# Attention energies as full-array float32r matmuls: keys and queries in two halves, keys read back from DRAM for every unit

## The chip, the core and the metric

The kernel runs on one core of a Trainium2 chip. The metric is device time in microseconds (us), from the first to the last instruction of the core. A core has TensorE (PE in the profile; PEld is its weight load), VectorE (DVE), ScalarE (ACT), GpSimd (POOL) and SyncE (SP, which here only issues transfers), and 16 DMA engines that all queues share.

## The reference: what is computed

Two layers on a tensor x of 4 images, 64 x 64 pixels, 256 channels, all in float32. The first is self-attention over the 4096 pixels of each image, with keys and queries of only 32 channels. The second is a DCNv3 block (layer norm, depthwise convolution, deformable sampling in 16 groups with 9 points each, projection) and an MLP with 1024 hidden channels. The change lies in the first layer:

```python
q = x @ wq + bq            # (4, 4096, 32)
k = x @ wk + bk            # (4, 4096, 32)
v = x @ wv + bv            # (4, 4096, 256)
energy = jnp.einsum('bnd,bmd->bnm', q, k)
attention = jax.nn.softmax(energy, axis=-1)
x_out = jnp.einsum('bnm,bmc->bnc', attention, v)
return gamma * x_out + inputs
```

## The kernel before, in words

**Tiling.** The work is cut into 64 *units* of 256 query pixels, 16 for each of the 4 images. For a unit, the energies of its 256 queries with all 4096 keys are made in 4 groups (`energies(g)`, line 743) of 8 matmuls, each for 128 keys x 256 queries with a contraction of 32 channels. A group fills four PSUM tiles `e0` to `e3` of 128 x 512. ScalarE turns them into exponentials (`exponentials`, line 756, four activations a group), without the row maximum. `weighted` (line 768) then multiplies the exponentials with the values V of the 4096 keys and accumulates the 256 x 256 result in PSUM; a column of ones in V gives the sum that the softmax divides by (`front`, lines 791 to 797).

**Keys and queries.** `project(b, u)` makes keys, queries and values of the 256 pixels of unit u of image b. `wkq` holds the weights of keys and queries side by side, in two orders, one for even and one for odd u, so that one pair of matmuls (`pkq`, line 651) gives keys and queries on the partitions where they are wanted. `key_bias` adds the bias on ScalarE: two activations of 32 x 128 put the keys into one of the four 32-partition strips of `kTs` (line 659), and one of 32 x 256 makes the queries (line 665), which SP writes to DRAM (`qd`, line 666). `kTs` has two sets of tiles in SBUF: while the units of one image are worked on, the other set receives the keys of the next image. `Attention.load` reads a unit's queries back four times, once for each strip (line 707). So four energies at a time run in four strips of 32 rows of the array.

**Other stages.** Around the attention, each unit passes `front` (residual, layer norm, input projection `pp`, line 825, written to DRAM as `xp`), `plan` (convolution, offsets and masks: the matmuls `po` at line 909, VectorE's `om` at line 918), `sample` (5 rows `win` of `xp` from DRAM, line 1068, weighted on VectorE, line 1088) and `back` (output projection `pout`, line 1169, then the MLP: `ph`, line 1194, and `pmlp`, line 1211). Several units are under way at once.

**Order.** The order of the work on TensorE, VectorE, ScalarE and GpSimd is written out by hand: every step has a due time in the table `WHEN` (a unit's period is T = 60 there), with other times for the last units in `LATE`. `whole` sorts all steps by due time and emits them; within an engine they run in that order. SP's transfers are not under that order; the framework places them. For the first image all 16 projections run ahead of the first unit; the projections for image b + 1 run during image b, one per unit.

A second version of the main loop (`general=True`, with `largest`) subtracts the row maximum and is only run when a check at the end finds values out of range. It was not run here.

Of the kernel before, what the change touches and what calls it, by code (L numbers as in the profile page):

```python
# [7 lines left out]

F32 = mybir.dt.float32
I32 = mybir.dt.int32  # L10
AF = mybir.ActivationFunctionType
ALU = mybir.AluOpType
AX = mybir.AxisListType
# [3 lines left out]
def tile_attention_dcnv3_block(  # L17
# [23 lines left out]
    nc = tc.nc  # L41
    B, H, W, C = x.shape
    N = H * W
    P = 128
# [88 lines left out]
    raw = p1.tile([P, C // P, 2, CQ], F32, tag="cv", name="raw_qk")  # L133
    for i, w in enumerate((wk, wq)):
        nc.sync.dma_start(raw[:, :, i, :], w.rearrange("(k p) m -> p k m", p=P))
    wkq, bkq = [], []
    for odd in range(2):
        t = const.tile([P, C // P, 4, CQ], F32, name=f"wkq{odd}")
        v = const.tile([P, 1], F32, name=f"bkq{odd}")
        for r in range(4):  # L140
            i = (r // 2 + odd) % 2
            nc.vector.tensor_copy(t[:, :, r, :], raw[:, :, i, :])
            nc.scalar.dma_start(v[r * CQ : (r + 1) * CQ, :], (bk, bq)[i].rearrange("(p o) -> p o", o=1))
        wkq.append(t.rearrange("p k r m -> p k (r m)"))
        bkq.append(v)
    wv_s = weight(wv, "wv_s", True)
    bv_s = bcast(bv, C, "bv_s", True)
    gamma_s = bcast(gamma, 1, "gamma_s")
# [174 lines left out]
    def rows4(r):  # L323
        return slice(r * CQ, (r + 1) * CQ)
# [293 lines left out]
    def project(b, u):  # L618


        n = f"{b}_{u}"
        first = b == 0
        odd = u % 2
        st = {}

        def load():
            if first:
                xs = p8.tile([P, 2, C], F32, tag="ex", name=f"xs_{n}")
            else:
                xs = p1.tile([P, C // P, 256], F32, tag="xs", name=f"xs_{n}")  # L630
            st["xs"] = xs
            if first:
                nc.sync.dma_start(xs, xt_[b, u])
            else:
                in_blocks(xs, xs_, b * N + 256 * u, 2)

        def turn():
            st["pt"] = transposed(st["xs"], f"x_{n}", 2, *((ps_e, f"e{odd}") if first else ()))

        def copy():  # L640
            st["xT"] = p3.tile([P, C // P, 256], F32, tag="cT", name=f"xT_{n}")
            if first:
                nc.scalar.copy(st["xT"], st["pt"])
            else:
                nc.vector.transpose(st["xT"].rearrange("p k t -> p (k t)"), st["xs"].rearrange("p k t -> p (k t)"))

        def keys():
            pool, tag = (ps_e, f"e{2 + odd}") if first else (ps, "m")
            st["pkq"] = pkq = pool.tile([P, 256], F32, tag=tag, name=f"pkq_{n}")
            for k in range(C // P):  # L650
                nc.tensor.matmul(  # L651
                    pkq, lhsT=wkq[odd][:, k, :], rhs=st["xT"][:, k, :], start=(k == 0), stop=(k == 1)
                )
# [36 lines left out]
        if not first:  # L690
            del d["turn"]
        return d
# [5 lines left out]
    class Attention:  # L698
        def __init__(self, b, u, general):
            self.b, self.u, self.general, self.n = b, u, general, f"{b}_{u}"  # L700
            self.ex = {}
            self.kT = kTs[b % 2]

        def load(self):
            self.qs = p2.tile([P, 256], F32, tag="qs", name=f"qs_{self.n}")
            for r in range(4):
                nc.sync.dma_start(self.qs[rows4(r), :], qd[self.b * NU + self.u])
            self.x = p2.tile([P, 2, C], F32, tag="x1", name=f"x1_{self.n}")
            nc.sync.dma_start(self.x, xt_[self.b, self.u])

        def e_tile(self, r, name):
            return ps_e.tile([P, 2, 256], F32, tag=f"e{r}", name=f"{name}_{self.n}")

        def largest(self):

            n, qs = self.n, self.qs
            self.nm = p2.tile([P, 256], F32, tag="qT", name=f"nm_{n}")
            for i in range(2):
                mxs = sm.tile([P, NT], F32, tag="mxs", name=f"mxs_{n}_{i}")
                for t in range(NT):  # L720
                    e = self.e_tile(t % 4, f"em_{i}_{t}")[:, 0, :P]
                    nc.tensor.matmul(
                        e, lhsT=qs[rows4(t % 4), i * P : (i + 1) * P], rhs=self.kT[t // 4][rows4(t % 4), :],
                        start=True, stop=True,
                    )
# [3 lines left out]
                nc.vector.tensor_scalar(  # L729
                    spread.rearrange("p (r c) -> p r c", c=CQ)[:, :, 0],  # L730
                    mx.to_broadcast([P, 4]), -1.0, None, ALU.mult,
                )
                pm = ps.tile([P, P], F32, tag="m", name=f"pm_{n}_{i}")
                nc.tensor.matmul(pm, lhsT=spread, rhs=ident, start=True, stop=True)
                nc.vector.tensor_copy(self.nm[:, i * P : (i + 1) * P], pm)

        def energies(self, g):
            if g == 0 and self.general:
                self.largest()
            self.es = es = [self.e_tile(r, f"e_{g}_{r}") for r in range(4)]  # L740
            for jj in range(2):
                for r in range(4):
                    nc.tensor.matmul(  # L743
                        es[r][:, jj, :], lhsT=self.kT[2 * g + jj][rows4(r), :], rhs=self.qs[rows4(r), :],
                        start=True, stop=not self.general,
                    )
                    if self.general:
                        nc.tensor.matmul(
                            es[r][:, jj, :], lhsT=every[rows4(r), :], rhs=self.nm[rows4(r), :],
                            start=False, stop=True,  # L750
                        )

        def exponentials(self, g):
            for r in range(4):
# [641 lines left out]
    def whole(general):  # L1396
        shifted.clear()
        wns, sps = {}, {}
        steps = []

        def put(slot, stage, some, later=0.0):
            late = LATE.get(stage, {}).get(slot, {})
# [4 lines left out]
        for b in range(B):  # L1407
            for u in range(NU):
# [11 lines left out]
                if general and u == 0:  # L1420
                    put(s, "general", {"e0": some.pop("e0"), "x0": some.pop("x0")})
                put(s, "attention", some)
                put(s, "tables", {k: lambda f=f: ready(f) for k, f in TABLES.items()})
# [96 lines left out]
```

## Time and profile before

| | |
|---|---|
| three runs, us | 3818.03, 3818.6, 3821.02 (median 3818.6) |
| profiled execution: span, us | 3820.9 (the page gives no other time of it) |
| energies (line 743), TensorE busy, us | 296.3 in 4096 records |
| weighted values (line 768), TensorE busy, us | 1902.2 in 8192 records |
| granted TensorE clock, mean over the span | 0.996 |
| DMA | 378.04 MB, 99 GB/s on average |
| spacing of units: images 1 to 3 / last image, us | 57.77 / 55.19 |

The page describes one profiled execution. Busy times are per engine; a record is one instruction. A float32 matmul shows as two records on PE and two on PEld. Matmuls are pipelined, so a record's duration is longer than the distance to the next one, and costs on TensorE are read as distances between starts. In a timeline line stand: start in us, duration in us, engine, line, operation, output <- inputs, shapes, number of records merged, and in brackets the idle time before it and what ended it.

### The profile page before, as it was taken

What the parts mean: (1) busy time and instruction counts of PE and PEld (TensorE: products, weight loads), DVE (VectorE), ACT (ScalarE), POOL (GpSimd) and SP (SyncE); (2) the same over time, 40 slices, a digit from 0 to 9 for tenths busy, and PEclk for the clock granted to TensorE, in tenths of its full rate; (3) what the DMA queues carried; (4) which work ended last, traced back from release to release, by engine and by line L of the source; (5) the groups of instructions that cost most, each with busy time, mean ns of one, the idle gap of its engine ahead of it and who ended that gap; (6) DMA issues with size and microseconds to landing.
All of it is one profiled execution on the core that took longest, in us unless ns stands there. A gap on an engine that the chain in (4) does not pass through costs nothing.

```text
span 3820.9 us, 56101 instructions
## 1 busy us (share of the span) xinstructions
PE 3773.3 (99%) x20274; PEld 3124.5 (82%) x20274; DVE 3422.7 (90%) x6247; ACT 2175.1 (57%) x4213; POOL 313.1 (8%) x444
## 2 busy tenths in 40 slices
PE   8999999999999999999999999999999999999988
PEld 7788888888888888888888888888888888888867
DVE  2599999999999999999999999999999999999995
ACT  4455555565565565565565565565565665555443
POOL 1000000000000000000000000000000000000021
PEclk9999999999999999999999999999999999999999
DMA  5333333334343333433534333333344333333331
GB/s 151 91 92 95 101 89 96 101 90 140 99 115 89 105 92 91 107 92 91 150 90 114 102 90 97 99 92 98 101 125 108 95 83 94 91 86 82 93 89 51
DMA packets 320111, 378.04 MB, mean 99 GB/s; under 512 B 133488, under 2 KB 270256, under 8 KB 319824
## 3 DMA queue, kind: packets, MB, share of 16 engines
q1 hardware_dynamic: 309728, 367.47, 35.5%
q10 hardware_dynamic: 8512, 3.43, 0.4%
q8 instruction: 162, 2.65, 0.3%
q0 software_dynamic: 1584, 3.47, 0.3%
q14 instruction: 125, 1.02, 0.1%
HBM read 251.69 MB, written 122.56 MB: 98 GB/s over the span
## 4 chain that ended last, share of the span: by engine, by line
PE 96%; DVE 3%; DMA 0%; ACT 0%; issue 0%; SPq 0%; ACTq 0%; DVEq 0%
PE acc L768 46%; PE ph L1194 12%; PE pmlp L1211 11%; PE e L743 7%; PE po L909 5%; PE pout L1169 3%; PE pp L825 3%; PE pv L672 3%; PE pkq L651 1%; PE pt_s L331 1%; PE pt_p L331 1%; PE pc L885 1%; DVE pw L1088 1%; PE pt_f L331 1%; PE pt_b L331 1%; DVE cv L872 1%
## 5 line engine op out<-in xcount | busy, mean ns | idle before, releaser
L768 PE MATMUL acc<-V,ex 128*128 128x257 f32 x8192 | 1902.2, 382 | 0.2
L768 PEld LDWEIGHTS acc<-V,ex 128*128 128x128 f32 x8192 | 1536.8, 190 | 267.4 <-issue 64.8
L1088 DVE TENSOR_TENSOR pw<-win,wn 128x1280 f32<-128x1280 f32 x640 | 933.2, 1484 | 9.5 <-ACT wn L1032 1.9
L1096 DVE TENSOR_TENSOR pw<-pw,pw 128x1280 f32<-128x1280 f32 x492 | 730.6, 1485 | 0.1
L756 ACT ACTIVATE ex<-e 128x512 f32<-128x512 f32 x1024 | 529.2, 603 | 64.5 <-PE e L743 55.7
L1194 PE MATMUL ph<-hT_b,f1w 128*128 128x256 f32 (+1 forms) x2080 | 494.0, 380 | 5.2 <-ACT hT_b L311 2.3
L1211 PE MATMUL pmlp<-f2w,gT 128*128 128x256 f32 x2048 | 462.7, 379 | 1.3 <-DVE x1b L1176 1.1
L1194 PEld LDWEIGHTS ph<-hT_b,f1w 128*128 128x128 f32 x2080 | 382.3, 190 | 81.9 <-issue 21.2
L872 DVE SCALAR_TENSOR_TENSOR cv<-hs,dw,cv 128x256 f32<-128x256 f32 (+1 forms) x1076 | 425.7, 465 | 1.4 <-ACT cv L868 1.3
L1211 PEld LDWEIGHTS pmlp<-f2w,gT 128*128 128x128 f32 x2048 | 384.2, 190 | 51.8 <-DVE x1b L1176 1.4
L1202 ACT ACTIVATE gT<-ph,f1b 128x256 f32<-128x256 f32 (+1 forms) x520 | 236.1, 467 | 256.4 <-PE ph L1194 254.7
L303 ACT ACTIVATE xn_p<-pc,nm_p,rstd_p 128x256 f32<-128x256 f32 x128 | 65.3, 560 | 555.9 <-DVE nm_p L295 553.1
L743 PE MATMUL e<-qs,kT 32*128 32x256 f32 x4096 | 296.3, 401 | 0.7 <-ACT ex L756 0.7
L743 PEld LDWEIGHTS e<-qs,kT 32*128 32x128 f32 x4096 | 186.8, 184 | 72.2 <-issue 62.9
L756 ACT ACT_TABLE_LOAD x182 | 233.5, 1283 | 3.2
L289 POOL TENSOR_SCALAR rstd_p<-mv_p 128x2 f32<-128x2 f32 (+1 forms) x65 | 76.2, 1173 | 1686.1 <-DVE mv_p L287 1614.5
L909 PE MATMUL po<-om_w,ge 128*128 128x432 f32 x512 | 196.6, 527 | 0.7 <-ACT ge L902 0.7
L998 DVE TENSOR_TENSOR pr<-hat 128x1296 f32<-128x1296 f32 x128 | 192.6, 1505 | 0.0
L1202 ACT ACT_TABLE_LOAD x124 | 159.1, 1283 | 2.2
L918 DVE TENSOR_TENSOR om<-po,om_b 128x432 f32<-128x432 f32 x128 | 77.2, 605 | 88.9 <-PE po L909 88.9
L902 ACT ACTIVATE ge<-pt_p,bd,gd 128x256 f32<-128x256 f32 (+1 forms) x130 | 65.9, 557 | 159.2 <-PE pt_p L331 159.2
L909 PEld LDWEIGHTS po<-om_w,ge 128*128 128x128 f32 x512 | 96.9, 190 | 71.1 <-issue 63.3
(220 smaller groups left out, 3839.5 us busy)
## 6 DMA issues: line engine op xcount, KB each, us to landing
win<-xp SPq DMA_DIRECT2D x536, 320.0 KB, 4.3
omd<-om SPq DMA_DIRECT2D x63, 432.0 KB, 2.5
x<-in_x_dram SPq DMA_DIRECT2D x64, 256.0 KB, 3.0
x1d<-x SPq DMA_DIRECT2D x64, 256.0 KB, 2.4
xp<-xq SPq DMA_DIRECT2D x128, 128.0 KB, 2.4
x1b<-x1d SPq DMA_DIRECT2D x63, 256.0 KB, 2.8
spd<-sp SPq DMA_DIRECT2D x63, 256.0 KB, 2.2
out_dram<-x1b SPq DMA_DIRECT2D x63, 256.0 KB, 3.0
```

Of the source, the lines that this page charges most:

```text
L331: nc.tensor.transpose(pt[:, k, i * P : (i + 1) * P], src[:, i, k * P : (k + 1) * P], ident)
L743: nc.tensor.matmul(es[r][:, jj, :], lhsT=self.kT[2 * g + jj][rows4(r), :], rhs=self.qs[rows4(r), :], start=True, stop=not self.general,)
L756: nc.scalar.activation(ex, self.es[r], AF.Exp)
L768: nc.tensor.matmul(self.acc[i], lhsT=ex[:, jj, i * P : (i + 1) * P], rhs=V[t // 2][:, t % 2, :], start=(g == 0 and r == 0 and jj == 0), st ...
L872: nc.vector.scalar_tensor_tensor(dst, src, dw[:, k, j : j + 1], dst, ALU.mult, ALU.add)
L909: nc.tensor.matmul(st["po", i], lhsT=st["ge"][:, k, i * P : (i + 1) * P], rhs=om_w[:, k, :], start=(k == 0), stop=(k == 1),)
L998: nc.vector.tensor_mul(pr.rearrange("p a b c d g -> p a b (c d g)"), hat[:, :, i, 1, :].unsqueeze(1).to_broadcast([P, 3, 3, S]), hat[:, :, ...
L1088: nc.vector.tensor_mul(st[r].rearrange("p d (g c) -> p (d g) c", c=GC), src.rearrange("p d (g c) -> p (d g) c", c=GC), wns[v][:, i, r] .re ...
L1096: nc.vector.tensor_add(st[0], st[0], st[r])
L1194: nc.tensor.matmul(ph[:, :m], lhsT=f1w[:, k, c * P : (c + 1) * P], rhs=st["hT"][:, k, :m], start=(k == 0), stop=(k == 1),)
L1202: nc.scalar.activation(st["gT"][:, c, :m], st["ph", c][:, :m], AF.Gelu, bias=f1b[:, c : c + 1])
L1211: nc.tensor.matmul(po, lhsT=st["gT"][:, c, i * P : (i + 1) * P], rhs=f2w[:, c, :], start=(c == 0), stop=(c == NH - 1),)
```

## The change

`project` now uses one weight order (key, query, key, query). `key_bias` makes, on partitions 0 to 63 (32 keys, 32 queries), a high half in float32r by one ScalarE activation, and a low half, the exact sum minus the high half, by one VectorE operation. Both halves of the keys are written to a DRAM tile `kd` (64 rows: high, low), both halves of the queries to `qd`: four writes instead of one. `kTs` is gone. A new step `keys(g)` reads the 64 rows of 1024 keys twice, into partitions 0 to 63 and 64 to 127 of a tile `kT` with two buffers, once for each unit and group (two transfers of 256 KB). The queries are read back as high, high, low, low. One full-array float32r matmul with a contraction of 128 then gives high x high + low x high + high x low + low x low. The two matmuls for one PSUM tile now follow one another. `whole` emits `keys(g)` 0.6 time units after the group two before it, which frees the buffer.

The core of the diff (what is left out concerns the version with the row maximum):

```diff
-    wkq, bkq = [], []
-    for odd in range(2):
-        t = const.tile([P, C // P, 4, CQ], F32, name=f"wkq{odd}")
-        v = const.tile([P, 1], F32, name=f"bkq{odd}")
-        for r in range(4):
-            i = (r // 2 + odd) % 2
-            nc.vector.tensor_copy(t[:, :, r, :], raw[:, :, i, :])
-            nc.scalar.dma_start(v[r * CQ : (r + 1) * CQ, :], (bk, bq)[i].rearrange("(p o) -> p o", o=1))
...
+    wkq = const.tile([P, C // P, 4, CQ], F32, name="wkq")
+    bkq = const.tile([P, 1], F32, name="bkq")
+    for r in range(4):
+        nc.vector.tensor_copy(wkq[:, :, r, :], raw[:, :, r % 2, :])
+        nc.scalar.dma_start(bkq[r * CQ : (r + 1) * CQ, :], (bk, bq)[r % 2].rearrange("(p o) -> p o", o=1))
...
-    kTs = [[kv.tile([P, P], F32, name=f"kT{i}_{j}") for j in range(NT // 4)] for i in range(2)]
-    qd = dram.tile([UN, CQ, 256], F32, name="qd")
+    qd = dram.tile([UN, 2, CQ, 256], F32, name="qd")
+    kd = [dram.tile([2 * CQ, N], F32, name=f"kd{b}") for b in range(B)]
...
         def key_bias():
-            pkq = st["pkq"]
-            for i in range(2):
-                rows = rows4(2 * odd + i)
-                nc.scalar.activation(
-                    kTs[b % 2][u // 2][rows, :], pkq[rows, i * P : (i + 1) * P], AF.Identity,
-                    bias=bkq[odd][rows, :],
-                )
-            rows = rows4(2 - 2 * odd)
-            qT = p2.tile([P, 256], F32, tag="qT", name=f"qT_{n}")
-            nc.scalar.activation(qT[rows, :], pkq[rows, :], AF.Identity, bias=bkq[odd][rows, :])
-            nc.sync.dma_start(qd[b * NU + u], qT[rows, :])
+            pkq, rows = st["pkq"], slice(0, 2 * CQ)
+            hi, lo = (p2.tile([P, 256], F32, tag="qT", name=f"kq{i}_{n}") for i in range(2))
+            nc.scalar.activation(hi[rows, :].bitcast(F32R), pkq[rows, :], AF.Identity, bias=bkq[rows, :])
+            nc.vector.scalar_tensor_tensor(
+                lo[rows, :].bitcast(F32R), pkq[rows, :], bkq[rows, :], hi[rows, :], ALU.add, ALU.subtract
+            )
+            for i, part in enumerate((hi, lo)):
+                nc.sync.dma_start(kd[b][i * CQ : (i + 1) * CQ, 256 * u : 256 * (u + 1)], part[:CQ, :])
+                nc.sync.dma_start(qd[b * NU + u, i], part[CQ : 2 * CQ, :])
...
             for r in range(4):
-                nc.sync.dma_start(self.qs[rows4(r), :], qd[self.b * NU + self.u])
+                nc.sync.dma_start(self.qs[rows4(r), :], qd[self.b * NU + self.u, r // 2])
...
+        def keys(self, g):
+            kT = kv.tile([P, 8, P], F32, tag="kT", bufs=2, name=f"kT_{self.n}_{g}")
+            for r in range(2):
+                nc.sync.dma_start(
+                    kT[64 * r : 64 * (r + 1)].rearrange("p t k -> p (t k)"),
+                    kd[self.b][:, 8 * P * g : 8 * P * (g + 1)],
+                )
+            self.kT[g] = kT.bitcast(F32R)
...
-            for jj in range(2):
-                for r in range(4):
+            for r in range(4):
+                for jj in range(2):
                     nc.tensor.matmul(
-                        es[r][:, jj, :], lhsT=self.kT[2 * g + jj][rows4(r), :], rhs=self.qs[rows4(r), :],
+                        es[r][:, jj, :], lhsT=self.kT[g][:, 4 * jj + r, :], rhs=self.qs.bitcast(F32R),
                         start=True, stop=not self.general,
                     )
...
+            for i, (_, fn) in enumerate(groups):
+                if i < 2:
+                    u = 4 * i + 3
+                    t = 3.6 * u - 1.8 + WHEN["attention"]["e0"] + WHEN["first"]["key_bias"] - T
+                else:
+                    t = groups[i - 2][0]
+                steps.append((t + 0.6, len(steps), fn))
```

More of the change, by code (lines that the diff above doesn't have):

```diff
@@ L10 @@
 I32 = mybir.dt.int32
+F32R = mybir.dt.float32r
 AF = mybir.ActivationFunctionType
@@ L135, in tile_attention_dcnv3_block @@
         nc.sync.dma_start(raw[:, :, i, :], w.rearrange("(k p) m -> p k m", p=P))
-    wkq, bkq = [], []
-    for odd in range(2):
-        t = const.tile([P, C // P, 4, CQ], F32, name=f"wkq{odd}")
-        v = const.tile([P, 1], F32, name=f"bkq{odd}")
-        for r in range(4):
-            i = (r // 2 + odd) % 2
-            nc.vector.tensor_copy(t[:, :, r, :], raw[:, :, i, :])
-            nc.scalar.dma_start(v[r * CQ : (r + 1) * CQ, :], (bk, bq)[i].rearrange("(p o) -> p o", o=1))
-        wkq.append(t.rearrange("p k r m -> p k (r m)"))
-        bkq.append(v)
+    wkq = const.tile([P, C // P, 4, CQ], F32, name="wkq")
[3 more added lines that the diff above has]
+        nc.scalar.dma_start(bkq[r * CQ : (r + 1) * CQ, :], (bk, bq)[r % 2].rearrange("(p o) -> p o", o=1))
+    wkq = wkq.rearrange("p k r m -> p k (r m)")
     wv_s = weight(wv, "wv_s", True)
@@ L651, in keys @@
                 nc.tensor.matmul(
-                    pkq, lhsT=wkq[odd][:, k, :], rhs=st["xT"][:, k, :], start=(k == 0), stop=(k == 1)
+                    pkq, lhsT=wkq[:, k, :], rhs=st["xT"][:, k, :], start=(k == 0), stop=(k == 1)
                 )
         def key_bias():
-            pkq = st["pkq"]
-            for i in range(2):
-                rows = rows4(2 * odd + i)
-                nc.scalar.activation(
-                    kTs[b % 2][u // 2][rows, :], pkq[rows, i * P : (i + 1) * P], AF.Identity,
-                    bias=bkq[odd][rows, :],
-                )
-            rows = rows4(2 - 2 * odd)
-            qT = p2.tile([P, 256], F32, tag="qT", name=f"qT_{n}")
-            nc.scalar.activation(qT[rows, :], pkq[rows, :], AF.Identity, bias=bkq[odd][rows, :])
-            nc.sync.dma_start(qd[b * NU + u], qT[rows, :])
+            pkq, rows = st["pkq"], slice(0, 2 * CQ)
[7 more added lines that the diff above has]
+                nc.sync.dma_start(qd[b * NU + u, i], part[CQ : 2 * CQ, :])
         def values():
@@ L701, in __init__ @@
             self.ex = {}
-            self.kT = kTs[b % 2]
+            self.kT = {}
         def load(self):
@@ L714, in largest @@
         def largest(self):
-            n, qs = self.n, self.qs
+            n, qs = self.n, self.qs.bitcast(F32R)
             self.nm = p2.tile([P, 256], F32, tag="qT", name=f"nm_{n}")
@@ L720, in largest @@
                 for t in range(NT):
+                    if t % 8 == 0:
+                        self.keys(t // 8)
                     e = self.e_tile(t % 4, f"em_{i}_{t}")[:, 0, :P]
                     nc.tensor.matmul(
-                        e, lhsT=qs[rows4(t % 4), i * P : (i + 1) * P], rhs=self.kT[t // 4][rows4(t % 4), :],
+                        e, lhsT=qs[:, i * P : (i + 1) * P], rhs=self.kT[t // 8][:, t % 8, :],
                         start=True, stop=True,
@@ L728, in largest @@
                 nc.vector.tensor_reduce(mx, mxs, AX.X, ALU.max)
[L729 to L732, printed above, removed]
+                nc.vector.tensor_scalar(spread[:, 0:1], mx, -1.0, None, ALU.mult)
                 pm = ps.tile([P, P], F32, tag="m", name=f"pm_{n}_{i}")
@@ L737, in energies @@
         def energies(self, g):
-            if g == 0 and self.general:
-                self.largest()
+            if self.general:
+                if g == 0:
+                    self.largest()
+                self.keys(g)
             self.es = es = [self.e_tile(r, f"e_{g}_{r}") for r in range(4)]
-            for jj in range(2):
-                for r in range(4):
+            for r in range(4):
+                for jj in range(2):
                     nc.tensor.matmul(
-                        es[r][:, jj, :], lhsT=self.kT[2 * g + jj][rows4(r), :], rhs=self.qs[rows4(r), :],
+                        es[r][:, jj, :], lhsT=self.kT[g][:, 4 * jj + r, :], rhs=self.qs.bitcast(F32R),
                         start=True, stop=not self.general,
@@ L747, in energies @@
                     if self.general:
[L748 to L751, printed above, removed]
+                        nc.tensor.matmul(es[r][:, jj, :], lhsT=every, rhs=self.nm, start=False, stop=True)
         def exponentials(self, g):
@@ L1398, in whole @@
         wns, sps = {}, {}
-        steps = []
+        steps, groups = [], []
         def put(slot, stage, some, later=0.0):
@@ L1422, in whole @@
                 put(s, "attention", some)
+                late = LATE["attention"].get(s, {})
+                groups += [
+                    (s * T + late.get(f"e{g}", WHEN["attention"][f"e{g}"]), lambda g=g, att=att: att.keys(g))
+                    for g in range(4)
+                ]
                 put(s, "tables", {k: lambda f=f: ready(f) for k, f in TABLES.items()})
```

## The prediction

> **What bounds the kernel now.** I read the busy line and the chain first, then the groups, then one steady stretch of the timeline on TensorE and on VectorE, then the transfers. The page:
>
> ```profile
> PE 3773.3 (99%) x20274; PEld 3124.5 (82%) x20274; DVE 3422.7 (90%) x6247; ACT 2175.1 (57%) x4213; POOL 313.1 (8%) x444
> ...
> PE 96%; DVE 3%; DMA 0%; ACT 0%; issue 0%; SPq 0%; ACTq 0%; DVEq 0%
> ...
> L768 PE MATMUL acc<-V,ex 128*128 128x257 f32 x8192 | 1902.2, 382 | 0.2
> L743 PE MATMUL e<-qs,kT 32*128 32x256 f32 x4096 | 296.3, 401 | 0.7 <-ACT ex L756 0.7
> ```
>
> TensorE is busy 99%, carries 96% of the chain, and in the waits it waits for nobody between 500 and 3500 us. So time taken from its queue comes off the end, until VectorE (90%) takes over. The energies (line 743) are 4096 records: 64 units x 4 groups x 8 matmuls, two records each. Their mean of 401 ns is a latency; what a group costs must be read from one start to the next:
>
> ```profile
> 2005.71 1.03 PE L1194 MATMUL ph<-hT_b,f1w 128*128 128x256 f32 x4
> 2006.67 1.15 PE L743 MATMUL e<-qs,kT 32*128 32x256 f32 x16
> 2007.74 2.00 PE L768 MATMUL acc<-V,ex 128*128 128x257 f32 x8
> 2009.58 3.62 PE L1211 MATMUL pmlp<-f2w,gT 128*128 128x256 f32 x16
> 2013.03 1.90 PE L768 MATMUL acc<-V,ex 128*128 128x257 f32 x8
> 2014.77 0.60 PE L885 MATMUL pc<-ident,cv 128*128 128x128 f32 x4
> 2015.20 3.62 PE L1211 MATMUL pmlp<-f2w,gT 128*128 128x256 f32 x16
> 2018.75 1.15 PE L743 MATMUL e<-qs,kT 32*128 32x256 f32 x16
> 2019.83 2.00 PE L768 MATMUL acc<-V,ex 128*128 128x257 f32 x8
> 2021.67 1.03 PE L651 MATMUL pkq<-xT,wkq 128*128 128x256 f32 x4
> 2022.53 1.90 PE L768 MATMUL acc<-V,ex 128*128 128x257 f32 x8
> ```
>
> The eight energies run from 2006.67 to 2007.74: 1.07 us. Their neighbours pay too: four records of 256 columns take 0.86 (2021.67 to 2022.53), but 0.96 just before energies; eight of 257 columns take 1.74 (2013.03 to 2014.77), but 1.84 just after. So a group costs **1.07 + 0.10 + 0.10 = 1.27 us**. It repeats every 57.77 us (2006.67, 2064.44). VectorE's waits for TensorE in the same unit:
>
> ```profile
> 2015.40 0.76 DVE L285 BATCH_NORM_STATS2 st_p<-pc 128x6 f32<-128x256 f32 x2 [0.31 <-PE pc L885]
> 2018.86 0.69 DVE L1217 TENSOR_TENSOR x1b<-x1b,pmlp 128x512 f32<-128x512 f32 x1 [1.10 <-PE pmlp L1211]
> 2028.09 0.61 DVE L918 TENSOR_TENSOR om<-po,om_b 128x432 f32<-128x432 f32 x1 [1.41 <-PE po L909]
> 2036.44 0.69 DVE L1176 TENSOR_TENSOR x1b<-x1b,pout 128x512 f32<-128x512 f32 x1 [0.49 <-PE pout L1169]
> ```
>
> and the room it has, in one unit of the first three images and in a stretch of the last one (time, then busy time of PE, PEld, DVE, ACT, POOL, then clock and DMA):
>
> ```profile
> 2064.44:2122.20 57.76, 57.76 (x313) 48.00 (x312) 53.47 (x96) 33.78 (x65) 4.41 (x6) 1.00 0.36 96
> 3206.00:3263.00 57.00, 57.00 (x310) 47.31 (x309) 54.02 (x96) 32.58 (x62) 4.41 (x6) 1.00 0.32 87
> ```
>
> VectorE is free 4.3 us of 57.76, in the last image 2.9 of 55.19 (the spacing of the groups there).
>
> **What the Trainium skill says.** (1) "FP8 and Floating Point Precision", TensorE Precision Notes: true FP32 takes four passes through the array, "FP32 reduced precision" truncates a 4-byte read. It gives no rate for float32r. The trace agrees on the four: a record costs 1.74 / 8 = 0.217 us for 257 columns and 0.362 for 432 (po, 2.90 us for eight), 0.83 ns a column, and a matmul is two records. (2) "TensorEngine Tiling (Array Packing)", Key Properties: changing the tiling mode drains TensorE. The 0.10 on either side of a group agrees. (3) "TensorE: Matmul & The Clock Gate", LDWEIGHTS: loading takes columns / 1.2 ns whatever the rows, 107 ns for 128. The four transposes at 2014.77 take 0.43 us, 0.108 per load and matmul, so the trace bounds it there.
>
> **The change, part by part.**
> *Energies.* 16 row-tiled records become 8 full-array ones. If float32r makes one of the four passes, 256 columns take 2 x 0.217 / 4 x 256/257 = 0.108 us, which the weight load just keeps up with (0.108). A group: 8 x 0.108 = **0.87 us**, no mode change. Saved 1.27 - 0.87 = 0.40, x 256 groups = **102 us**. The trace shows no float32r. Bounds: below, one pass and nothing else, 102 us saved; above, two cycles a column as each present record has, 8 x 0.216 = 1.73 us, +0.46 x 256 = 118 us lost. Break-even is 1.27 / 8 = 0.159 us a matmul. I take one pass: two records of two cycles a column are the four passes that (1) gives to full precision, and a truncated read has no low halves for the other three.
> *Bias step, ACT.* Two 356 ns activations and one of 465 become one of about 465: 0.71 us less per unit, on an engine at 57%. Worth 0.
> *Bias step, VectorE.* One more operation per unit, 64 x 256 from PSUM; nearest row is line 797 (477 ns, 128 x 256 from PSUM). 64 x 0.48 = 31 us. It waits for ACT's high half, and the whole VectorE queue behind it. In the trace ACT starts this step at 2025.81, so the high half is there by 2026.3; VectorE then reaches the 1.41 us gap ahead of om. It fits: 0, or 48 x 0.48 = 23 us if the gap is gone (startup's 16 apart; the last image has none).
> *Key loads.* Two of 256 KB for each of 256 groups: 512 issues, 134 MB. The nearest row:
>
> ```profile
> q1 hardware_dynamic: 309728, 367.47, 35.5%
> win<-xp SPq DMA_DIRECT2D x536, 320.0 KB, 4.3
> ```
>
> 134 / 367 x 35.5% adds 13 points of DMA time, 49% in all. With 0.486 us an issue (win's median) and three more small writes at 0.30, SP gets 8 x 0.49 + 3 x 0.30 = 4.8 us more per unit, while it waits for VectorE some 14 us at a stretch. A buffer is free when group g-2 has run, and its load is wanted at group g: 2006.67 to 2033.33 is 26.7 us, 25 to 31 for the others, 11.4 at the least near the end (3552.14 to 3563.59). Two issues and a 4.3 us landing make 5.3. Hidden: 0; if SP sits in one of its 14 us waits ahead of the load, still inside 25. What queues behind a key load on SP is window rows, x, vd and qs; a load that waits for group g-2 could hold them, but TensorE has run that group some 25 us before the data is needed. Value 0, upper end 10 us, in the last units.
> *Startup.* Sixteen projections at 3.03 us apiece (pkq at 31.15 and 34.18), now with four writes each and one ring of two buffers: high half 0.47, issue 0.36 twice, landing 1.5, so about 2.9 against 3.03, and the first key loads wait on SP for the writes. Fewer weight copies and bias loads take off about 1. Value +3, from -1 to +12.
> *What is late next.* Of the 1.60 us saved per unit, two groups (0.80) fall between the divisions (line 791) and st_p, where VectorE has 0.31 of wait; it falls 0.5 behind and gets it back at x1b (1.10). In the last image the waits are 0.96, 0.54, 0.48 and 0.23, with 0.60 for GpSimd that stays: 2.2 for 1.6 saved. That is tight, and I give back a third: 16 x 0.5 = 8 us. After 3630 us no energies run, and the end there is set by VectorE and latencies: 0; but its order was laid for other times: +3.
>
> Sum: -102 + 0 + 3 + 8 + 3 = **-88 us**. The page gives the profiled execution no time besides its span, 3820.9, which equals the slowest of the three times (3821.02) within 0.1, and is 2.3 above their median. 3820.9 - 88 = 3732.9; on the median, 3818.6 - 88 = **3730.6**.
>
> **Rivals.** *VectorE keeps half.* What it cannot win back behind st_p (0.80 - 0.31 = 0.49 x 48 = 24 us), and the whole saving of the last image past its 2.2 us less 0.48 for the new operation's queueing (another 10), go lost: 3731 + 34 = 3765. For it: 90% busy. Against: its waits are spread and larger than the savings between them. *Two cycles a column* (ends slower): float32r halves the passes by its weights only and streams as now. 3818.6 + 118 = 3937, a little less where VectorE is waiting already: 3930. For it: every record in this trace has two cycles, the one-record transposes too, as far as 0.108 for 128 columns can tell. Against: a weight load would explain those just as well. It decides from 0.159 us a matmul on. *The type changes nothing*: two records of the full array per matmul, 8 x 0.43 = 3.46 us a group, +2.19 x 256 = 560: 4380. Unlikely, since by (1) it is full precision that takes four passes.
>
> **Chances.** One pass and hidden 0.62 (3712 to 3752), VectorE keeps half 0.18 (3750 to 3785), two cycles 0.13, nothing changes 0.03, no difference 0.02, under 3712 0.02. A measurement tells about 0.2% (8 us) from no change. Faster 0.82, same 0.02, slower 0.16. Range 3710 to 3785: the first two cases, 0.80; it holds startup's -1 to +12, the 23 us of the new VectorE operation and the loads' 10.
>
> **What would show it.** Groups of 8 energy records, 0.87 us from the first to what follows, and no 0.10 before or after: units 56.2 us apart instead of 57.77. No wait of TensorE for the key tile. VectorE's wait at st_p gone, that at om down to about 0.5. DMA near 49%. If the starts inside a group are 0.21 apart, the second rival is right; if they are 0.11 apart but units stay above 57 us, VectorE or SP took it, and TensorE's waits name which.

## The result, and the profile after

| | before | after |
|---|---|---|
| median of 4 runs each, us | 3819.36 (3818.03 to 3821.02) | **3755.22** (3754.62 to 3759.17) |
| ratio, with 95% interval | | **0.9833** (0.9819 to 0.9847) |
| span of the profiled execution, us (its own time) | 3820.9 (3821.02) | 3753.7 (3755.45) |
| spacing of units, images 1 to 3 / last image, us | 57.77 / 55.19 | 56.48 / 53.89 |

The kernel is faster by 64 us (1.7%) on the medians, and by 67.2 on the spans of the two profiled executions; 88 had been forecast. The page of the kernel after, the lines that answer to those of before:

```profile
PE 3693.6 (98%) x18226; PEld 3185.1 (85%) x18226; DVE 3442.1 (92%) x6307; ACT 2122.0 (57%) x4085; POOL 313.1 (8%) x444
...
q1 hardware_dynamic: 359904, 508.02, 51.9%
...
L774 PE MATMUL acc<-V,ex 128*128 128x257 f32 x8192 | 1887.0, 380 | 0.0
...
L752 PE MATMUL e<-qs,kT 128*128 128x256 f32 x2048 | 321.7, 300 | 0.0
```

The energies are now 2048 records, one for a matmul, where a float32 matmul shows two. Their busy time went *up* from 296.3 to 321.7 us: the four strips of before overlapped and were counted once. The line tells nothing of the gain. That is read from one start to the next on TensorE, in the timeline of the kernel after:

```profile
2031.54 1.03 PE L1200 MATMUL ph<-hT_b,f1w 128*128 128x256 f32 x4
2032.22 1.30 PE L752 MATMUL e<-qs,kT 128*128 128x256 f32 x8
2033.35 1.89 PE L774 MATMUL acc<-V,ex 128*128 128x257 f32 x8
2035.09 3.62 PE L1217 MATMUL pmlp<-f2w,gT 128*128 128x256 f32 x16
2038.54 1.90 PE L774 MATMUL acc<-V,ex 128*128 128x257 f32 x8
2040.27 0.60 PE L891 MATMUL pc<-ident,cv 128*128 128x128 f32 x4
2040.71 3.62 PE L1217 MATMUL pmlp<-f2w,gT 128*128 128x256 f32 x16
2043.98 1.30 PE L752 MATMUL e<-qs,kT 128*128 128x256 f32 x8
2045.12 1.90 PE L774 MATMUL acc<-V,ex 128*128 128x257 f32 x8
```

A caution: the first energy record is shown some 0.18 us before its neighbour's time is over, so the group is costed together with that neighbour. From ph to acc are 2033.35 - 2031.54 = 1.81 us; four ph records take 4 x 0.216 = 0.86; **0.95 us** is left for the energies. From pmlp to acc, 2045.12 - 2040.71 = 4.41 less 16 x 0.216 = 3.45 leaves 0.96. The acc behind takes 1.74, the same as far from energies, so the 0.10 on either side of a group is gone. Before, a group cost 1.27.

VectorE's waits for TensorE in the same unit:

```profile
2041.17 0.75 DVE L285 BATCH_NORM_STATS2 st_p<-pc 128x6 f32<-128x256 f32 x2
2044.36 0.69 DVE L1223 TENSOR_TENSOR x1b<-x1b,pmlp 128x512 f32<-128x512 f32 x1 [0.85 <-PE pmlp L1217]
2053.27 0.61 DVE L924 TENSOR_TENSOR om<-po,om_b 128x432 f32<-128x432 f32 x1 [0.70 <-PE po L915]
2061.30 0.69 DVE L1182 TENSOR_TENSOR x1b<-x1b,pout 128x512 f32<-128x512 f32 x1 [0.16 <-PE pout L1175]
```

The wait at st_p is gone, the other three shrank (1.10 to 0.85, 1.41 to 0.70, 0.49 to 0.16): 1.60 us less in a unit, for 1.29 saved on TensorE and a new operation of 0.47 on VectorE. One unit, and one of the last image (columns as in the prediction's lines on VectorE's room):

```profile
2032.22:2088.70 56.48, 56.48 (x283) 48.92 (x281) 53.77 (x98) 32.87 (x63) 4.41 (x6) 1.00 0.57 144
3141.94:3195.82 53.88, 53.88 (x270) 46.64 (x269) 52.18 (x94) 32.50 (x63) 4.40 (x6) 1.00 0.50 130
```

TensorE is still busy throughout; VectorE has 2.7 us left in a unit and 1.7 in the last image.

The startup is where time was lost. The first and the last energies before, and after:

```profile
66.72 1.15 PE L743 MATMUL e<-qs,kT 32*128 32x256 f32 x16
...
3625.62 1.15 PE L743 MATMUL e<-qs,kT 32*128 32x256 f32 x16
```

```profile
81.00 3.38 PE L752 MATMUL e<-qs,kT 128*128 128x256 f32 x16
...
3557.41 1.30 PE L752 MATMUL e<-qs,kT 128*128 128x256 f32 x8
```

**Where 67.2 us come from:** first energies 14.3 later; from there to the start of the last ones 3557.41 - 81.00 = 3476.4 instead of 3625.62 - 66.72 = 3558.9, 82.5 less; and 1.0 more behind them (196.3 instead of 195.3). Four groups per unit at 0.32 less are 1.28, the 1.29 that the units lost; 256 x 0.32 = 82. So all that TensorE saves arrives at the end.

### The profile page after: what moved, and what is told of

Its sections match the earlier page's. It is cut to its first block, busy times and chain, and to the rows that moved or that the text cites. A ratio compares the mean times of both kernels' runs of the same rounds, so it can differ in the third digit from the quotient of the medians.

```text
span 3753.7 us, 53218 instructions
## 1 busy us (share of the span) xinstructions
PE 3693.6 (98%) x18226; PEld 3185.1 (85%) x18226; DVE 3442.1 (92%) x6307; ACT 2122.0 (57%) x4085; POOL 313.1 (8%) x444
## 3 DMA queue, kind: packets, MB, share of 16 engines
q1 hardware_dynamic: 359904, 508.02, 51.9%
## 4 chain that ended last, share of the span: by engine, by line
PE 89%; DVE 5%; issue 0%; DMA 0%; ACT 0%; POOL 0%; DVEq 0%; SPq 0%; ACTq 0%; POOLq 0%
PE acc L774 43%; PE pmlp L1217 11%; PE ph L1200 11%; PE e L752 6%; PE po L915 5%; PE pout L1175 3%; PE pp L831 3%; PE pv L670 2%; DVE pw L1094 1%; PE pkq L651 1%; DVE cv L878 1%; DVE pw L1102 1%; PE pt_s L331 1%; PE pt_b L331 1%; PE pt_p L331 1%; PE pc L891 1%
## 5 line engine op out<-in xcount | busy, mean ns | idle before, releaser
L752 PE MATMUL e<-qs,kT 128*128 128x256 f32 x2048 | 321.7, 300 | 0.0
L752 PEld LDWEIGHTS e<-qs,kT 128*128 128x128 f32 x2048 | 271.4, 190 | 8.1 <-ACT ex L762 0.8
L303 ACT ACTIVATE xn_b<-x1b,nm_b,rstd_b 128x256 f32<-128x256 f32 x128 | 70.0, 593 | 129.8 <-DVE nm_b L295 129.8
```

The source lines that it names most:

```text
L303: nc.scalar.activation(xn[:, i, :], s, AF.Identity, bias=nm[:, i : i + 1], scale=st["r"][:, i : i + 1])
L752: nc.tensor.matmul(es[r][:, jj, :], lhsT=self.kT[g][:, 4 * jj + r, :], rhs=self.qs.bitcast(F32R), start=True, stop=not self.general,)
```

## The experiments

Two theories went into the runs. **A**: a float32r matmul streams its columns in one pass of 0.46 ns each, and that alone is the gain; the key loads and VectorE's operation are hidden; what was lost was lost at startup, in the ring of the halves (two buffers used in turn, so that a new half waits until the writes of an older one are done). **B**, in several forms: something else takes the missing 20 us of the steady part (a fixed cost of a matmul or its weights, the order of the PSUM tiles, the traffic of the key loads, VectorE), or the gain comes from the full array and not from the type. The kernel before was run beside each batch (3820 to 3822 us).

### The type: float32 instead of float32r (e3_float32)

```diff
-F32R = mybir.dt.float32r
+F32R = mybir.dt.float32
```

> The change whole, with its halves and its matmuls of the energies in plain float32 instead of float32r (the high half is then the whole sum and the low half zero). Theory A (the number of passes sets the cost of a group: float32r streams its columns once, float32 four times in two records): 16 records of the full array in a group at 0.216 us each, 3.46 us a group against 0.95, so units 56.47 + 4 x 2.51 = 66.5 us apart, and 256 x 2.5 = 640 us more than the change: about 4390 us. Rival (the type does nothing, and it is the full array, the order and the end of the mode change that brought the 82 us): 8 records and 56.5 us, or 3755 us. In between (16 records of which the strips' end saves something else): units near 60.

Measured: **4376.92 us** (one run), and in its timeline:

```profile
2038.15 1.03 PE L1200 MATMUL ph<-hT_b,f1w 128*128 128x256 f32 x4
2039.02 3.62 PE L752 MATMUL e<-qs,kT 128*128 128x256 f32 x16
2042.47 1.90 PE L774 MATMUL acc<-V,ex 128*128 128x257 f32 x8
```

16 records in 2042.47 - 2039.02 = 3.45 us, units 66.50 apart. The type is the whole gain: without it, the kernel with the same full-array matmuls takes 557 us more than the one with strips. That float32 takes four passes is what the Trainium skill says ("FP8 and Floating Point Precision", TensorE Precision Notes); these traces come near it, with 3.45 us a group against 0.95 for float32r, 3.6 times.

### Where does 0.119 us per matmul come from? (e2_wide, e6_rows_outer, e10_bf16)

e2_wide gives each matmul 512 columns (the unit's queries twice) and halves their number:

```diff
             for r in range(4):
+                if not self.general:
+                    nc.tensor.matmul(
+                        es[r], lhsT=self.kT[g][:, r, :],
+                        rhs=self.qs.bitcast(F32R).unsqueeze(1).to_broadcast([P, 2, 256]),
+                        start=True, stop=True,
+                    )
+                    continue
                 for jj in range(2):
```

> Four energy matmuls of 512 columns a group instead of eight of 256: each uses its keys against the unit's queries twice, so half of the keys are left out and the others count twice. Theory A (the weight load sets the 0.119 us of a matmul; the columns alone would take 0.108 for 256): 0.215 us a matmul, 0.86 us a group instead of 0.95, units 0.36 us closer (56.1), 23 us less, 3732. Theory B (the columns stream at 0.465 ns each): 0.238 us a matmul, 0.95 a group, units still 56.47, 3755.

Measured: 3753.15 us, ratio 0.982 (0.9803 to 0.9836), units 56.44 apart (2033.81 to 2090.25).

```profile
2033.14 1.03 PE L1207 MATMUL ph<-hT_b,f1w 128*128 128x256 f32 x4
2033.81 1.27 PE L752 MATMUL e<-qs,kT 128*128 128x512 f32 x4
2034.92 1.90 PE L781 MATMUL acc<-V,ex 128*128 128x257 f32 x8
```

From ph to acc 1.78, less 0.86: 0.92 for four matmuls, 0.23 each. The same reading at a unit's other three groups gives 0.93 to 0.94, where the kernel after has 0.95 to 0.96. So half as many matmuls and weight loads, with twice the columns each, take nearly the same time: the columns set most of it. Only some 0.02 of the 0.08 us that a group takes beyond the forecast go with the number of matmuls.

e6_rows_outer only swaps the two loops, so that a group's matmuls go around the four PSUM tiles as before:

```diff
-            for r in range(4):
-                for jj in range(2):
+            for jj in range(2):
+                for r in range(4):
```

> The changed kernel with the old order of the eight energies: the four PSUM tiles in turn, so that no two matmuls in a row write the same tile. Theory A (float32r streams a column in 0.46 ns by itself, as the wide run says): group 0.95 us, units 56.47, 3755. Theory B (writing one PSUM tile twice in a row costs the 0.011 us a matmul over 0.108): group 0.87, units 56.15, 3734.

Measured: 3755.44 us, ratio 0.9832 (0.9815 to 0.9848), units 56.48. The order of the PSUM tiles is worth nothing.

e10_bf16 keeps the halves in bfloat16:

```diff
-F32R = mybir.dt.float32r
+F32R = mybir.dt.bfloat16
...
-    qd = dram.tile([UN, 2, CQ, 256], F32, name="qd")
+    qd = dram.tile([UN, 2, CQ, 256], F32R, name="qd")
...
-            kT = kv.tile([P, 8, P], F32, tag="kT", bufs=2, name=f"kT_{self.n}_{g}")
+            kT = kv.tile([P, 8, P], F32R, tag="kT", bufs=2, name=f"kT_{self.n}_{g}")
```

> The change with its halves kept in bfloat16 instead of float32r: the two halves of keys and queries, their DRAM tiles, the key tile and the queries' tile. It leaves out the digits of the low half that bfloat16 does not hold; the number of matmuls, of columns and of transfers is the change's, the transfers have half the bytes. It asks where 0.119 us for a matmul of 256 columns comes from, when a quarter of a float32 matmul would be 0.108. Theory A (float32r has a column rate of its own, a tenth slower than a quarter of float32's): in bfloat16 a group takes 8 x 0.108 + little = 0.86 us, units 56.47 - 4 x 0.09 = 56.1 us apart, 256 x 0.09 = 22 us less than the change, about 3733 us. Theory B (something outside the type, such as a fixed cost of each matmul or PSUM's side, sets 0.119): units stay 56.47, 3755 us. Startup may gain a microsecond or two in both cases, since its writes are halved.

Measured: 3743.42 us, ratio 0.9801 (0.9785 to 0.9817).

```profile
2037.05 1.04 PE L752 MATMUL e<-qs,kT 128*128 128x256 bf16 x8
2037.92 1.90 PE L774 MATMUL acc<-V,ex 128*128 128x257 f32 x8
...
2061.27 1.04 PE L752 MATMUL e<-qs,kT 128*128 128x256 bf16 x8
2062.15 1.96 PE L1200 MATMUL ph<-hT_b,f1w 128*128 128x256 f32 x8
2063.95 1.90 PE L774 MATMUL acc<-V,ex 128*128 128x257 f32 x8
```

A group takes 0.87 us here, 0.109 a matmul: near the 0.108 that the prediction had put for float32r. So the missing tenth comes with the type. The units did not follow in full: they are 56.32 apart (2004.95 to 2061.27) instead of the expected 56.1. Of 4 x 0.08 = 0.32 us about half is lost, and the matmuls behind two of the four groups show where: the ph above takes 1.80 us for eight records (2062.15 to 2063.95) instead of 8 x 0.216 = 1.73, and the pout behind another group 1.79 (2052.11 to 2053.90). From first to last energies the kernel gained 9.1 us on the kernel after (78.00 to 3545.34), at startup 3.0, at the end 1.5: 13.6, the difference of the spans. The 3.0 is no more than the spread among kernels with the same startup (see e1_three_halves).

### What hides the rest of the change? (e4_few_loads, e5_no_low_op)

e4_few_loads loads keys twice per image instead of four times per unit:

```diff
-                        es[r][:, jj, :], lhsT=self.kT[g][:, 4 * jj + r, :], rhs=self.qs.bitcast(F32R),
+                        es[r][:, jj, :], lhsT=self.kT[g if self.general else g % 2][:, 4 * jj + r, :], rhs=self.qs.bitcast(F32R),
...
+                    if u == 0 and g < 2:
+                        groups.append((b, g, lambda g=g, att=att: att.keys(g)))
```

> The key tile is loaded twice per image instead of four times per unit: groups 2 and 3 use the keys of groups 0 and 1, so half of the keys are left out and the others count twice. 496 of the 512 load transfers are gone. Theory A (the key loads are hidden): units 56.47 us apart as in the changed kernel, 3755 within 5; DMA time falls from 52% to near 38%. Theory B (the loads cost time, by SyncE's queue or by contention with the other transfers): units closer than 56.4, 3745 or less.

Measured: 3755.11 us, ratio 0.9825 (0.9808 to 0.9841), with the first queue at

```profile
q1 hardware_dynamic: 320224, 377.96, 37.7%
```

and units of 56.48 us. The loads, 130 MB and 14 points of DMA time, cost nothing in the steady part, and do not slow the float32r columns either.

e5_no_low_op puts a constant zero tile for the low half and drops VectorE's operation:

```diff
-            hi, lo = (p2.tile([P, 256], F32, tag="qT", name=f"kq{i}_{n}") for i in range(2))
+            hi, lo = p2.tile([P, 256], F32, tag="qT", name=f"kq0_{n}"), no_low
...
-            nc.vector.scalar_tensor_tensor(
-                lo[rows, :].bitcast(F32R), pkq[rows, :], bkq[rows, :], hi[rows, :], ALU.add, ALU.subtract
-            )
```

> VectorE's low-half operation is left out: the low halves are zeros, still written and read. The high half then has both buffers of its ring. Theory A (the operation is hidden behind VectorE's waits in the steady part): units still 56.47 us apart; only the startup gets shorter, as with more buffers, first energies near 68 us, 3742. Theory B (VectorE is the next limit): units 0.2 to 0.45 us closer, 3725 to 3735.

Measured: 3745.87 us, ratio 0.9802 (0.9785 to 0.9818).

```profile
69.97 3.46 PE L751 MATMUL e<-qs,kT 128*128 128x256 f32 x16 [5.59 <-DMA qs<-qd]
```

Units stay at 56.48 (53.88 in the last image), with VectorE's busy time down to 3417.9. All its gain is at startup, where one tile per projection lets the ring hold two projections: 11.0 us earlier. From the first energies to the end it is 3671.7 us, against 3672.7 for the change. The operation is hidden in the steady part.

### The startup (e1_three_halves, e8_startup_ring, e9_startup_queue)

In the kernel after, the first 16 projections wait for their own writes. Its waits (us in total, times, longest), TensorE's and ScalarE's:

```profile
PE pkq L651 <- DVE kq L659: 11.1, 5, 3.8
...
ACT kq L658 <- DMA qd<-kq: 49.0, 14, 10.0
```

One round on ScalarE and on SP's queue, and the longest stall of this stretch:

```profile
44.23 0.47 ACT L658 ACTIVATE kq<-pkq,bkq 64x256 fp32r<-64x256 f32 x1 [6.55 <-DMA qd<-kq]
48.11 0.47 ACT L658 ACTIVATE kq<-pkq,bkq 64x256 fp32r<-64x256 f32 x1 [2.94 <-DMA qd<-kq]
51.35 0.47 ACT L658 ACTIVATE kq<-pkq,bkq 64x256 fp32r<-64x256 f32 x1 [2.22 <-DMA qd<-kq]
```

```profile
37.19 1.21 SPq L713 DMA_DIRECT2D kT<-kd  x2
38.49 0.53 SPq L663 DMA_DIRECT2D kd<-kq  x1
39.07 0.41 SPq L664 DMA_DIRECT2D qd<-kq  x1
...
48.61 0.30 SPq L663 DMA_DIRECT2D kd<-kq  x1
48.95 0.42 SPq L664 DMA_DIRECT2D qd<-kq  x1
```

The high half is ready at 48.58, its second write is issued from 48.95 on, and the buffer is free, with the next high half starting, at 51.35: 2.4 us from the start of that issue, for writes that land in a median of 2.0. This round is 3.24 us long, just over the 3.03 of a projection before. Where a pair of key loads stands ahead of the writes (37.19), the same write, from 39.07, frees the buffer only at 44.23: 5.2 us later. From one high half to the next, the 13 rounds from 28.64 to 79.53 take 3.9 us on average; the two with key loads in their way take 7.5 (36.75 to 44.23) and 5.3 (54.89 to 60.17), the others 2.5 to 4.5. Thirteen times 3.9 - 3.03 is 11 of the 14.3 us.

e1_three_halves gives the ring a third buffer:

```diff
-            hi, lo = (p2.tile([P, 256], F32, tag="qT", name=f"kq{i}_{n}") for i in range(2))
+            hi, lo = (p2.tile([P, 256], F32, tag="qT", bufs=3, name=f"kq{i}_{n}") for i in range(2))
```

> The changed kernel with three buffers instead of two for the halves of keys and queries. Theory A (the ring of two buffers sets the pace of the first image's projections: each waits for the writes of the one before): the first energies come near 70 us instead of 81.0, ScalarE's waits for the writes of the halves shrink from 49 us to under 20, and the time falls by about 11 us, to 3744. Theory B (SyncE is the limit there: four writes a projection, and key loads that wait for writes hold the queue): first energies still near 80 us, 3755 as the changed kernel. Units stay 56.47 us apart in both.

Measured: 3750.09 us, ratio 0.9812 (0.9796 to 0.9829), units 56.48.

```profile
76.11 3.42 PE L752 MATMUL e<-qs,kT 128*128 128x256 f32 x16 [2.76 <-DMA qs<-qd]
```

The first energies come 4.9 us earlier, less than half of what A expected; ScalarE's waits for the writes fell from 49.0 to 15.5. (In e2, e3, e4, e6 and e7, whose startup has the steps and the ring of the kernel after, the first energies come between 77.90 and 80.80; 76.11 lies below all of them.) One buffer more does not hold a second projection, so e8_startup_ring takes eight, in the tile of another stage that is idle then:

```diff
-            hi, lo = (p2.tile([P, 256], F32, tag="qT", name=f"kq{i}_{n}") for i in range(2))
+            if first:
+                if not halves:
+                    halves.append(gp.tile([P, NH, 256], F32, tag="gT", name="halves"))
+                hi, lo = (halves[0][:, 2 * (u % 4) + i, :] for i in range(2))
+            else:
+                hi, lo = (p2.tile([P, 256], F32, tag="qT", name=f"kq{i}_{n}") for i in range(2))
```

> The changed kernel, with a ring of four projections for the halves of the first image, in a tile that is idle then. Theory A (the ring): first energies near 70 us as in the run without the low-half operation, limited there by the late load of the first queries, 3744. Theory B (VectorE's operation, which is back here, holds the projections): first energies at 76 as with three buffers, 3750. Units 56.47 in both.

Measured: **3745.72 us**, ratio 0.9805 (0.9789 to 0.9821), units 56.48; ScalarE's waits for the writes are down to 7.3.

```profile
70.60 3.75 PE L759 MATMUL e<-qs,kT 128*128 128x256 f32 x16 [5.20 <-DMA qs<-qd]
```

10.4 us of the 14.3 are back with VectorE's operation in its place, so what e5_no_low_op gained came from the ring and not from that operation. Of the versions that do the whole work of the change, this one and e9 are the fastest. What is left is the wait for the first queries. In the kernel before they went through DRAM too, and no energies waited for them; here SP issues their load only at 64.47 us, behind the writes of the halves.

e9_startup_queue is e8 with the high halves' writes issued by ScalarE's queue:

```diff
-                nc.sync.dma_start(kd[b][i * CQ : (i + 1) * CQ, 256 * u : 256 * (u + 1)], part[:CQ, :])
-                nc.sync.dma_start(qd[b * NU + u, i], part[CQ : 2 * CQ, :])
+                queue = nc.scalar if first and i == 0 else nc.sync
+                queue.dma_start(kd[b][i * CQ : (i + 1) * CQ, 256 * u : 256 * (u + 1)], part[:CQ, :])
+                queue.dma_start(qd[b * NU + u, i], part[CQ : 2 * CQ, :])
```

> As the run before, and the first image's high halves are written from ScalarE's queue instead of SyncE's, which leaves SyncE two writes a projection. Theory A (SyncE's queue is what delays the load of the first queries): no wait for them, first energies near 65 us, 3739. Theory B (ScalarE, now issuing 32 transfers of some 0.4 us, becomes the limit of the startup): first energies at 72 or later, 3746 or more.

Measured: 3745.48 us, ratio 0.9804 (0.9788 to 0.982): no more than e8.

```profile
69.13 1.29 PE L760 MATMUL e<-qs,kT 128*128 128x256 f32 x8
72.10 1.97 PE L760 MATMUL e<-qs,kT 128*128 128x256 f32 x8 [1.68 <-ACT ex L770]
```

The wait for the queries is gone (their loads are issued from 42.4 us on), but ScalarE, which now issues as well, is late with the first exponentials: one wait took the other's place.

### Strips in float32r (e7_strips)

```diff
-            for r in range(4):
-                for jj in range(2):
+            for jj in range(2):
+                for r in range(4):
+                    rows = slice(0, P) if self.general else rows4(r)
                     nc.tensor.matmul(
-                        es[r][:, jj, :], lhsT=self.kT[g][:, 4 * jj + r, :], rhs=self.qs.bitcast(F32R),
+                        es[r][:, jj, :], lhsT=self.kT[g][rows, 4 * jj + r, :], rhs=self.qs[rows, :].bitcast(F32R),
```

> Float32r in the old four strips of 32 rows: only the high halves are multiplied, the three products with low halves are left out. It separates the pass from the change of tiling mode. Theory A (the mode change costs as before, and a pass of four strips runs at once in 0.119 us): two rounds instead of four of 0.215 us, 1.27 - 4 x 0.215 + 2 x 0.119 = 0.65 us a group, units 55.3 us apart, about 3680. Theory B (float32r runs one strip at a time): 8 x 0.119 + 0.41 = 1.36 us a group, units 58.1, about 3860.

What the edit computes is not what the expectation says. The key tile holds high, low, high, low on its four strips and the queries' tile high, high, low, low, so each strip makes a different one of the four products, and only the first is high by high. The shapes and the number of matmuls, on which the time rests, are the ones meant.

Measured: 3722.16 us, ratio 0.9739 (0.9723 to 0.9755), units 55.84.

```profile
2015.47 1.03 PE L1201 MATMUL ph<-hT_b,f1w 128*128 128x256 f32 x4
2016.43 0.51 PE L753 MATMUL e<-qs,kT 32*128 32x256 f32 x8
2016.87 2.00 PE L775 MATMUL acc<-V,ex 128*128 128x257 f32 x8
...
2041.29 0.60 PE L331 MATMUL pt_s<-ident,sp 128*128 128x128 f32 x4
2041.82 0.51 PE L753 MATMUL e<-qs,kT 32*128 32x256 f32 x8
2042.56 1.99 PE L1176 MATMUL pout<-ow,sT 128*128 128x256 f32 x8 [0.24 <-ACT sT L1170]
...
2051.85 0.51 PE L753 MATMUL e<-qs,kT 32*128 32x256 f32 x8
2052.58 2.02 PE L1201 MATMUL ph<-hT_b,f1w 128*128 128x256 f32 x8 [0.21 <-ACT hT_b L311]
```

The first group is as A had it: 0.44 and the 0.10 of the mode change on either side, 0.64. But the unit lost 1.93 against the kernel before, not 4 x 0.63 = 2.5. In two of the four groups TensorE waits for a copy that ScalarE makes: 0.24 us for sT and 0.21 for hT_b. From the start of these energies to what follows are 0.74 and 0.73 us instead of 0.44, together 0.59 more, which is what the unit lacks. From 500 to 3500 us TensorE waits 52 times for each of the two copies, 23.6 us in all; in the kernel after it waits for neither there. Where the energies stand between a transpose and the matmul that wants its copy, they cover that copy: groups of 0.95 us do, groups of 0.44 do not. The ph and the pout that are slower in e10_bf16 stand at the same two places, but its trace shows no wait there, so that this is the cause in e10 too was not shown.

## Why the prediction was right, and where its sum was off

The side, the mechanism and the range held: float32r shows as one record, the mode change is gone, and all of TensorE's saving reached the end. The median is 24.6 us above the forecast. It lies 3 us above the 3712 to 3752 that the prediction gave its first case, and inside the 3750 to 3785 of the rival *VectorE keeps half*; the range held because it joined the two. On the spans the sum was -88 and the measured -67.2, term by term:

- **Energies, forecast -102, measured -82.5.** One record and no mode change: right (e3_float32 for the type; for the mode change, the 1.74 us of the acc behind a group, where it was 1.84). The Trainium skill says that a change of tiling mode drains TensorE ("TensorEngine Tiling (Array Packing)", Key Properties), and the 0.10 on either side comes back with the strips of e7_strips. The term failed in its size: "256 columns take 2 x 0.217 / 4 x 256/257 = 0.108 us" took float32r's pass for a quarter of a float32 matmul. It is 0.119, 0.46 ns a column; about the quarter, 0.109, is what bfloat16 takes (e10_bf16). Eight matmuls by 0.011, by 256 groups, are 22 us, near enough all of this term's miss. Why a float32r matmul takes a tenth longer stays open: at most a quarter of it goes with the number of matmuls and weight loads (e2_wide), and none with the order of the PSUM tiles (e6_rows_outer) or the traffic of the key loads (e4_few_loads). The prediction took the lower of two bounds (0.108 and 0.216 a matmul) and put no chance on a value between them.
- **Startup, forecast +3 (from -1 to +12), measured +14.3.** The place was named: a ring of two buffers. The size was not: "high half 0.47, issue 0.36 twice, landing 1.5, so about 2.9 against 3.03" (by its terms 2.7) took the landing from the one small write of before. With four writes, VectorE's step between them, and key loads of 256 KB on the same queue, the landing is 2.0 at the median and 6.3 at the most, and a round takes 3.9 on average. e8_startup_ring widens the ring and gets 10.4 back; the remaining 4 come with a wait for the load of the first queries, which stands behind the writes on SP's queue.
- **VectorE late, forecast +8, and the late order, +3: measured 0 and +1.0.** The last image's units lost 1.30 us, as much as the others, and VectorE has 1.7 us left in them; there was no need to give back a third. Its waits shrank and so took up the saving, and e5_no_low_op puts the new operation at 0 outside startup.
- **Bias step and key loads, forecast 0: right.** st_p's wait vanished and om's fell to 0.70 (0.5 was named). DMA's share is 51.9% for 49. A wait of the weight load for po behind VectorE's operation, 7.6 us in 44 times, was not foreseen; e5_no_low_op shows that it does not reach the end.
- The two misses upward, 19.5 and 11.3, less 10 given back too much, are the 20.8 us. So it is in part luck that the time stayed so near the forecast: an allowance that nothing used made up for a third of two misses elsewhere.

The rivals: *VectorE keeps half* was put at 3765 and is nearest in time. Its "another 10" does not come out of its own terms (2.2 less 0.48 is 1.72, more than the 1.6 saved); without it 3755 would have stood there, the measured time, by a cause that did not act. The time alone could not tell the two apart; the spacing of the units does, since nothing of TensorE's saving was lost (1.29 a unit, from four groups of 0.32). *Two cycles a column*, 1.73 us a group, is refuted by 0.95. *The type changes nothing*, put at 4380, is what e3_float32 ran: 4377. That it came so near is in part luck too: from first to last energies that run took 541 us more than the kernel before (77.90 to 4178.24), not 560, and 11 came from the startup, which the price left out.

## What to carry to other kernels

A float32 matmul whose operands are split into high and low float32r halves, stacked along an idle part of the contraction, took here little more than a quarter of the time of the same matmul in float32 (0.95 us a group instead of 3.45), but only 0.32 less than four float32 strips at once; in which of the two forms the work lies before the change decides how much the change is worth. When a stage's tiles begin to travel through DRAM, cost its *first* pass by itself: buffers that are free again in time at one per unit are not when sixteen follow one another, and a spare tile of an idle stage mended most of it (10.4 of 14.3 us). And when an edit shortens a group of matmuls, ask what the group was covering on the other engines: past that point the neighbours' copies become the limit.

## What the runs showed of the hardware

- float32r: 0.119 us for a matmul of 256 columns and 0.23 for 512 (0.46 ns a column), one record; bfloat16 0.109 for 256, one record; float32 0.43 in two records.
- In the trace float32r appears as `f32` on TensorE; the number of records (one for a matmul) and the mean of a record (300 ns against 379 for pmlp, both of 256 columns) tell them apart.
- Four 32-row strips in float32r run at once too: eight matmuls in 0.44 us (e7_strips), where eight of the full array take 0.95.
- The first record of a float32r group is shown up to 0.18 us before its predecessors' time is over, so a group has to be costed with its neighbour.
